# Row normalization and weight centring moved to ScalarE, one GpSimd task to VectorE, and a new order of steps, in a Nyström attention block with an expert FFN

## The chip, the cores and the metric

The kernel runs on one core of one Trainium2 chip. Such a core has five engines that run side by side, each working through its own instructions in order: TensorE (PE in the profile, its weight loads PEld), VectorE (DVE), ScalarE (ACT), GpSimd (POOL) and SyncE (SP), which here issues the DMA transfers. Engines wait for each other through semaphores. Matrix products land in PSUM, which other engines must empty before TensorE can write there again; everything else lies in SBUF.

The metric is the time of one execution in device microseconds. The kernel before was timed in three runs.

## The reference

The input is x of shape (16, 1024, 256) in float32: 16 batches of 1024 rows. Two sublayers follow each other, each with a normalization in front of it and one behind it:

```python
x = x + _layernorm(_L0_attn_ref(_layernorm(x), w_qkv, w_proj))
x = x + _layernorm(_L0_ffn_ref(_layernorm(x), W_base, b_base, Wd1, bd1, Wd2, bd2, Wa_down, ba_down, Wa_up, ba_up))
```

The attention has 16 heads of width 16 and 64 landmarks. Its landmarks are means over 16 neighbouring rows, and the inverse is an iteration of six steps:

```python
Q_l = Q.reshape(b, H, M, n // M, HD).mean(axis=-2)
K_l = K.reshape(b, H, M, n // M, HD).mean(axis=-2)
kernel1 = softmax(Q @ K_l^T); kernel2 = softmax(Q_l @ K_l^T); kernel3 = softmax(Q_l @ K^T)
SV = (kernel1 @ iterative_inv(kernel2)) @ (kernel3 @ V)
out = SV @ w_proj
```

The feed-forward part tries 8 small autoencoders (256 to 64 to 256) on the 1024 rows, picks the one with the least reconstruction loss, and adds that expert's adapter to a base projection. (The reference reads 16 batches of 1024 rows here; the loss is a mean over a batch's rows.)

```python
h = relu(x @ Wd1[e] + bd1[e]);  recon = h @ Wd2[e] + bd2[e]
losses = mean((recon - x) ** 2);  idx = argmin over e
a = relu(x @ Wa_down[idx] + ba_down[idx])
return x @ W_base + b_base + a @ Wa_up[idx] + ba_up[idx]
```

A layernorm here has no gain and no bias: (x - mean) / sqrt(var + 1e-5). Since the results of both sublayers are normalized again along the row, the kernel centres the weights that produce them (each row of `w_proj`, `W_base`, the chosen `Wa_up` and the bias rows loses its mean), so that the results have mean zero and only a variance is left to be found.

## The kernel before

Each batch passes four stages, written as Python generators. A generator yields at each *step*, and what stands between two yields is emitted in one piece.

- **Stage a** (`stage_a`, line 446): Q, K and V from the normalized rows. Steps `qk` (line 475: 64 matmuls each, two for Q and two for K; ScalarE copies at line 483, VectorE sums landmarks at line 489), `v` (line 500), `bd` (landmark matrices), `max` (line 547 with VectorE's maxima at line 556), `mcol` and `mrow` (the maxima split into three bfloat16 parts and turned), `e3` (lines 567 and 578, exponential on ScalarE at line 588), `ut` (line 604), `u`. The next batch's statistics and normalization (`stats` and `xn`) run inside it.
- **Stage p** (`stage_p`, line 664): the 64 by 64 inverse for all heads as one serial chain; `k2`, `k2n`, `sums`, `kv0`, then six rounds of `l` (line 698 and ScalarE's copy at line 780), `h` (VectorE, line 783) and `q` (line 698 and VectorE, line 787), then `end`.
- **Stage c** (`stage_c`, line 799): the queries' softmax (`max`: line 823 with VectorE's maxima at line 831; `mt`; `e1`: lines 862 and 870 with the exponential at line 880), the weighted values (`sv`: line 891), the projection (`po`: line 926), the residual addition (`out`: line 411). Its generator starts with the step `weights`, `prepare_c` (line 295), which centres `wproj_sb`.
- **Stage d** (`stage_d1` and `stage_d2`): statistics and normalization (`stats`, `xn`), the turn of the rows (`xt`), the eight experts (`ht`: line 999; `df`: line 1029, VectorE's difference at line 1037, two squares on ScalarE at line 1040), the choice (`pe`, `gather`, and an index read by SyncE that starts the loads of the expert's weights, `wup`), then `a`, `po` (line 1158) and `out`. Batch 0 starts with the step `weights`, `prepare_d` (line 302): three small transposes of bias rows on TensorE, three copies on ScalarE, and the centring of `wbase_sb` and the bias rows on VectorE.

Rows are normalized in `rows_normalized` (line 382), once per 512 rows: four tiles of 128 rows by 256, each by one `tensor_scalar` on VectorE (`normalized`, line 346). In stage a a VectorE transpose of the same 512 rows follows. The mean `mv` comes from VectorE (line 364), the reciprocal root `rstd` from two GpSimd instructions (`rstd_of`, line 367). There are 16 batches with two halves in each of two places: 64 such steps.

`in_parts` (line 338) splits float32 values into three bfloat16 parts with four instructions (copy, subtract, copy, subtract) on the engine that it is given; the queries' maxima in stage c are split on GpSimd (line 839).

Five streams of steps exist: stage a, stage p, stage c, stage d for all batches but the last but one, and stage d for that one. The string `ORDER` says which stream goes next; it has 1648 digits, and each engine gets its instructions in that order. The string `PAIRS` says which of four PSUM buffers (two banks each) every product takes, in the same order. Both were worked out ahead of time and are part of the program:

```python
order, emitted = [int(k) for k in ORDER], streams()
with tc.manual_schedule(engines={PE, Activation, DVE, Pool}):
    for k in order:
        next(emitted[k], None)
```

All loads and stores go through SyncE's queue in the order of emission. At the start it holds the first rows (8 transfers of 128 KB), `w_qkv` four times over (12 of 256 KB), `w_proj` four times over (4 of 256 KB), the experts' weights (1024 KB in three), `W_base` (256 KB), then the small bias rows and the rows for the base bias.

In stage d `spare` puts matmuls without use in front of a wait of the last batch (20 ahead of the transposes of batch 15, 16 ahead of its adapter).

Of the kernel before, what the change touches and what calls it, by code (L numbers as in the profile page):

```python
# [8 lines left out]
F32 = mybir.dt.float32  # L9
I32 = mybir.dt.int32  # L10
BF16 = mybir.dt.bfloat16
AF = mybir.ActivationFunctionType
ALU = mybir.AluOpType
X = mybir.AxisListType.X
PSUM = bass.MemoryType.PSUM

P = 128
# [1 line left out]
N_ITER = 6  # L19
PARTS = 3  # L20
ORDER = (
    "0000020000012000000000000011000000012110130011010010110121010110120101201100000122120122020000202012"
    "0112120112312013021310332001312132013303102333301301000133100030113003000330101102121023130112012213"
    "3201313001213030003201201000002133200020003312203013013023020111001022113212210302232033030100333133"
    "0133133310333333210313001012213311221030211331112100103322303030230200002312013003102223312301000133"
    "3313103333223133333130231300122133112213211030203001033221303030202033130010221022302331223133330321"
    "0333313010003333332103013001022131311221031021312330013322030302020012311100102303003022233113010001"
    "3331330210013313323233313330213123002122330001301233233322030301332331233132121331133231333331331223"
    "3331302003200210123021312010301200100020133200020003312203013033032331233132121333313321333311113333"
    "3202300122033211202133222101023010120100001010100101330001022303330302011203133112311120331231122133"  # L30
    "3322321333100110202130301230220113312013332031300000131312303030012013330303303311123123313212313332"
    "3112231333223213333101300131033110230132011003201200100020133200020001011223033303010200203023112030"
    "0302223312310100333132231010001333002210013322233321333211001330221030313113311130330200203232323300"
    "3122133223201201333331012013133313123331321233120332010313000010213001330012013330303303311110200112"
    "0012003102331300100033332232033323232333333211033101023032022302331001133230122033030113321323133123"
    "3113313213331313321212333331301120013011232132112321220102031020010033200330013023323302031211212223"
    "3231333131231133331323331321133122313122311312113121133212331224424422442224224422244444224244444442"
    "344423333334333443333343343333333433443333244333"
)
PAIRS = (  # L40
    "0123012301230123012301230123012301203120312032103120312031203120310321032013201320123102310321032103"
    "2013201323012301230123012301230123012301203120312013201320132013203120310231021032103210321032103231"
    "0231023102310231032103210321023102310231203120312031203120312031023102310231023012301203102310321023"
    "1023102310231203120132031203120312031203013203120310231021302103210321032103210321032103201320310231"
    "0231023102310213021320132013201320132013201312023103210320132013201320132013201320132013201302103210"
    "3210321032103210321032103210231023012301232031320132031203102301230123012301230123012310231023103210"
    "3210321032103201320123012301302130213021302102310213102310321032013201320132013210321032103210321032"
    "1032103120312031203120310231021032103212031203210321032103210321032103120312031230123012301230123012"
    "3102312031203120312031203123012301230123013201320132012301230123102310231023102310321032103210312031"
    "0231023102310231023102310231203120313201320132013120310231023120312031203120310231023103210321032103"  # L50
    "2103201320132013210321032103210321032103120312031203213021032103210321032103210321032103210321032103"
    "2130213012301230123012302132013203120123012301230123012132013201320132012301320132013203120312031203"
    "1203120132013201302130213021302130213012130213021302130213021030213032103201320132012301230120312031"
    "2031203120132013201320132103210231023102310231023102310232102310321032130213021302130213021302130213"
    "0123012301230132013201321032103210321032103210312301230123013210321032103120312031203120230123010231"
    "2031203120312031203120312031203102310231302103210321032103210321032013201320312031203120312031203102"
    "3102310231021302132012301230123021"
)


# [20 lines left out]
def kernel(  # L81
# [17 lines left out]
    nc = tc.nc  # L99
    NB, N, D = x.shape  # L100
# [3 lines left out]
    NC = D // P  # L104
    ND = D // 32
# [3 lines left out]
    E, _, R = wa_down.shape  # L109
# [20 lines left out]
    def rows32(p):  # L130
        return slice(32 * p, 32 * p + 32)
# [17 lines left out]
    def buf4k(tag, shape, name, bufs=2):  # L149

        return work.tile(shape, F32, tag=tag, name=name, bufs=bufs)
# [35 lines left out]
    wproj_sb = const.tile([P, ND, D], F32, name="wproj_sb")  # L187
# [67 lines left out]
    for c in range(NC):  # L255
        for r in range(2):
            j = 2 * c + r
# [37 lines left out]
    def prepare_c():  # L295
        yield go(("c", 0, "weights"), [("a", 0, "qk", 0, 0)])
        mean = small.tile([P, ND], F32, tag="means", name="means", bufs=1)
        nc.vector.tensor_reduce(mean, wproj_sb, X, ALU.add)
        nc.vector.tensor_scalar(mean, mean, 1.0 / D, None, ALU.mult)
        nc.vector.tensor_tensor(wproj_sb, wproj_sb, last(mean, D), ALU.subtract)  # L300

    def prepare_d():
        yield go(
# [39 lines left out]
            if q + 1 < PARTS:  # L343
                engine.tensor_copy(dst(q), rest)

    def normalized(dst, src, mv, rstd, i):
        nc.vector.tensor_scalar(dst, src, mv[:, i, 0:1], rstd[:, i : i + 1], ALU.subtract, ALU.mult)

    def go(name, follows):
        return name, follows

# [24 lines left out]
    def rows_normalized(b, at, src_of, stats, dst_of, turned_to=None):  # L382

        for h in range(NT // 4):
            yield go((at, b, "xn", h), [(at, b, "stats", h)])
            src, dst = src_of(h), dst_of(h)
            for j in range(4):
                normalized(dst[:, j, :], src[:, j, :], *stats[h], j)
            if turned_to is not None:
                nc.vector.transpose(  # L390
                    turned_to(h).rearrange("p (k t) c -> p t k c", t=4), dst.rearrange("p t (k c) -> p t k c", c=32)
                )
# [406 lines left out]
    def stage_c(b):  # L799
# [13 lines left out]
        def max_of(n, t0):  # L813

            if t0 == 0:
                most[n] = small.tile([P, 4, 4, 2 * NC], F32, tag="most1", name=f"most1_{b}_{n}", bufs=1)
            mx = most[n]
            psc = [two_banks([P, 2, 2, NC, P], f"psc1_{b}_{n}_{t0}_{g}") for g in range(PC // 2)]
            for c in range(NC):
                for t in range(2):  # L820
                    cols = slice((4 * n + t0 + t) * P, (4 * n + t0 + t + 1) * P)
                    for p in range(PC):
                        nc.tensor.matmul(  # L823
                            psc[p // 2][:, p % 2, t, c, :],
                            lhsT=qt[rows32(p), c, cols],
                            rhs=bd[rows32(p), NC + c, :, :].rearrange("f r l -> f (r l)"),
                            start=True,
                            stop=True,
                        )
            for g in range(PC // 2):  # L830
                nc.vector.tensor_reduce(  # L831
                    mx[:, t0 : t0 + 2, 2 * g : 2 * g + 2].rearrange("x t p j -> x p t j"),
                    psc[g].rearrange("x p t c (r l) -> x p t (c r) l", r=2),
                    X,
                    ALU.max,
                )
            if t0:
                by_row = maxima.rearrange("x t (p j) -> x t p j", p=4)
                in_parts(
                    nc.gpsimd, lambda q: by_row[:, :, :, q * 2 * NC : (q + 1) * 2 * NC], mx, mx  # L840
                )

        def before_rows(n):
# [364 lines left out]
    for k in order:  # L1208
        name, follows = stretches[k][place[k]]
# [50 lines left out]
```

## Time and profile before

| what | value |
|---|---|
| runs | 1941.35, 1941.46, 1944.79 us; median 1941.46 |
| profiled execution, time | 1940.27 us |
| profiled execution, span | 1938.1 us |
| mean granted TensorE clock | 0.99 |
| GpSimd busy | 212.1 us (11%) |
| moved by DMA | 64.30 MB, 33 GB/s over the span |
| first matmul starts at | 15.37 us |

The span is the time from the first to the last instruction in the profile; the execution takes 2.2 us more. Busy time is the time in which an engine executes; matmuls are pipelined, so that a busy TensorE isn't always one at its full rate. A line of a group reads: source line, engine, operation, tile written and read, shapes, count, then busy us in total and mean ns of one, then the idle time of the engine in front of these instructions and what ended it. A line of a timeline reads: start in us, length in us, engine, source line, operation, tiles, count, and in brackets the idle time of the engine before it and its releaser.

The largest groups outside TensorE are the squares of the reconstruction error on ScalarE (line 1040, 362.7 us) and the differences on VectorE (line 1037, 298.7 us), then VectorE's two maxima (lines 831 and 556, 150.2 and 149.8 us). One table load of ScalarE stands at the start (1.28 us).

### The profile page before, as it was taken

The page shows a single profiled execution, that of the slowest core. Times are in us where ns is not written, and L with a number is a line of the kernel's source. Part 1 is how long each engine was busy: PE and PEld are TensorE (multiplying, and loading weights), DVE is VectorE, ACT ScalarE, POOL GpSimd, SP SyncE. Part 2 cuts the span into 40 slices and gives each one's busy share as a digit, 9 for nine tenths or more (in the row PEclk, how much of TensorE's full clock was granted, in tenths as well). Part 3 has the DMA queues.
Part 4 walks back from the last instruction along what each step waited for, and adds up shares of the span by engine and source line. Part 5 has one row for each costly group of instructions (what it writes and reads, how often), then busy time and mean ns, then how long its engine had stood idle before and what let it go on. Part 6 is the DMA issues. An engine that isn't in the chain of part 4 may idle for free.

```text
span 1938.1 us, 81528 instructions
## 1 busy us (share of the span) xinstructions
PE 1844.0 (95%) x37175; PEld 1265.7 (65%) x37175; DVE 1511.4 (78%) x2805; ACT 1133.1 (58%) x2434; POOL 212.1 (11%) x423
## 2 busy tenths in 40 slices
PE   6789999999999999999999999999999999989898
PEld 5667578567585766677676666866758485755544
DVE  6787878878788787787788887888788877686664
ACT  1243745573847557665655756557474667456576
POOL 1001001001110101101010010101101010010101
PEclk9899999999999999999999999999999999999899
DMA  8011011102020110111110111110201110010101
GB/s 203 3 25 25 3 28 47 24 18 56 7 67 3 51 24 12 40 29 46 28 34 15 29 45 28 46 24 8 67 7 46 24 51 2 7 46 7 45 6 48
DMA packets 65767, 64.30 MB, mean 33 GB/s; under 512 B 9244, under 2 KB 65424, under 8 KB 65424
## 3 DMA queue, kind: packets, MB, share of 16 engines
q1 hardware_dynamic: 65424, 59.11, 11.7%
q8 instruction: 291, 4.77, 1.0%
q14 instruction: 52, 0.43, 0.1%
HBM read 42.32 MB, written 16.78 MB: 30 GB/s over the span
## 4 chain that ended last, share of the span: by engine, by line
PE 78%; DVE 11%; ACT 5%; issue 2%; DMA 2%; POOL 1%; SPq 1%; DVEq 0%; POOLq 0%; ACTq 0%
PE ph L999 10%; PE pq L475 10%; PE pr L1029 10%; PE pf L1158 6%; PE pv L500 5%; PE po L926 5%; PE psv L891 4%; PE psct L862 3%; PE psc L823 3%; PE psm L547 3%; PE pxl L698 3%; PE psc L578 3%; PE pxq L698 3%; PE put L604 2%; DVE mx L556 2%
## 5 line engine op out<-in xcount | busy, mean ns | idle before, releaser
L1040 ACT ACTIVATE df<-df,bd_sb 128x512 f32<-128x512 f32 x512 | 362.7, 711 | 80.8 <-DVE df L1037 80.6
L1037 DVE TENSOR_TENSOR df<-pr,xt_d 128x1024 f32<-128x1024 f32 x256 | 298.7, 1215 | 58.2 <-PE pr L1029 45.6
L475 PE MATMUL pq<-xa,wqkv_sb 32*128 32x256 f32 x4096 | 242.5, 382 | 15.6 <-DVE xa L390 15.4
L1029 PE MATMUL pr<-ht,wd_sb 64*64 64x512 f32 x2048 | 245.6, 599 | 1.0 <-ACT ht L1007 0.2
L999 PE MATMUL ph<-xt_d,wd_sb 128*128 128x512 f32 x512 | 236.5, 604 | 2.1 <-issue 0.9
L475 PEld LDWEIGHTS pq<-xa,wqkv_sb 32*128 32x128 f32 x4096 | 219.4, 187 | 28.9 <-DVE xa L390 15.4
L556 DVE TENSOR_REDUCE mx<-psm 128x2 f32<-128x1024 f32 x128 | 149.8, 1217 | 37.4 <-PE psm L547 36.9
L999 PEld LDWEIGHTS ph<-xt_d,wd_sb 128*128 128x128 f32 x512 | 92.0, 189 | 116.2 <-issue 94.4
L831 DVE TENSOR_REDUCE most<-psc 128x16 f32<-128x1024 f32 x128 | 150.2, 1216 | 14.1 <-PE psc L823 13.9
L880 ACT ACTIVATE e<-psct 128x1024 f32<-128x1024 f32 x128 | 123.8, 1019 | 60.9 <-PE psct L870 60.6
L1029 PEld LDWEIGHTS pr<-ht,wd_sb 64*64 64x64 f32 x2048 | 67.6, 132 | 120.5 <-issue 56.4
L588 ACT ACTIVATE e<-psc 128x1024 f32<-128x1024 f32 x128 | 122.9, 1025 | 31.4 <-PE psc L578 30.9
L926 PE MATMUL po<-wproj_sb,svn 32*128 32x256 f32 x2048 | 126.9, 380 | 1.5 <-DVE svn L962 1.4
L1007 ACT ACTIVATE ht<-ph,bd_sb 128x1024 f32<-128x1024 f32 x64 | 70.9, 1108 | 93.7 <-PE ph L999 93.5
L500 PE MATMUL pv<-wqkv_sb,xa 32*128 32x256 f32 x2048 | 124.7, 379 | 0.1
L926 PEld LDWEIGHTS po<-wproj_sb,svn 32*128 32x128 f32 x2048 | 108.7, 185 | 19.4 <-DVE df L1037 4.9
L1158 PE MATMUL pf<-wbase_sb,xt_d 128*128 128x256 f32 x512 | 120.0, 388 | 0.0
L500 PEld LDWEIGHTS pv<-wqkv_sb,xa 32*128 32x128 f32 x2048 | 109.3, 185 | 6.9 <-issue 1.0
L1158 PEld LDWEIGHTS pf<-wbase_sb,xt_d 128*128 128x128 f32 x512 | 95.3, 191 | 22.7 <-issue 10.9
L783 DVE SCALAR_TENSOR_TENSOR q<-qw,eye 128x512 f32<-128x512 f32 x96 | 65.2, 679 | 45.1 <-ACT qw L780 44.7
L787 DVE SCALAR_TENSOR_TENSOR xw<-xw,pxq 128x640 f32<-128x640 f32 x96 | 69.7, 726 | 39.2 <-PE pxq L698 38.4
L1040 ACT ACTIVATION_READ_ACCUMULATOR df<-df,bd_sb 128x1 f32 x512 | 96.7, 189 | 0.0
(185 smaller groups left out, 3054.7 us busy)
## 6 DMA issues: line engine op xcount, KB each, us to landing
x<-in_L_attn_x_dram SPq DMA_DIRECT2D x16, 1024.0 KB
xa<-in_L_attn_x_dram SPq DMA_DIRECT2D x60, 256.0 KB
out_dram<-y_d SPq DMA_DIRECT2D x30, 512.0 KB
wqkv_sb<-in_L_attn_w_qkv_dram SPq DMA_DIRECT2D x12, 256.0 KB
wup<-in_L_ffn_Wa_up_dram SPq DMA_DIRECT2D x30, 64.0 KB
xa<-in_L_attn_x_dram SPq DMA_DIRECT2D x8, 128.0 KB
wproj_sb<-in_L_attn_w_proj_dram SPq DMA_DIRECT2D x4, 256.0 KB
out_dram<-y_d SPq DMA_DIRECT2D x4, 256.0 KB
```

The source lines that it names most:

```text
L475: nc.tensor.matmul(pq[g // 2][:, g % 2, 0 : N // 4], lhsT=wqkv_sb[rows32(g), k, f0 : f0 + P], rhs=turned[rows32(g), k], start=(k == 0), st ...
L500: nc.tensor.matmul(pv[g // 2][:, g % 2, 0:D], lhsT=turned[rows32(g), k, t0 // 4, :], rhs=wqkv_sb[rows32(g), k, 2 * D : 3 * D], start=(k == 0),
L556: nc.vector.tensor_reduce(mx3[:, n, q : q + 2], psc[g], X, ALU.max)
L588: nc.scalar.activation(e, psc[g], AF.Exp)
L831: nc.vector.tensor_reduce(mx[:, t0 : t0 + 2, 2 * g : 2 * g + 2].rearrange("x t p j -> x p t j"), psc[g].rearrange("x p t c (r l) -> x p t ...
L880: nc.scalar.activation(e, psc[g], AF.Exp)
L926: nc.tensor.matmul(po[g // 2][:, g % 2, 0:D], lhsT=svt[rows32(g), k, :], rhs=wproj_sb[rows32(g), k, :], start=(k == 0), stop=(k == ND - 1),)
L999: nc.tensor.matmul(ph[:, n, :], lhsT=wd1_sb[:, k, 2 * i : 2 * i + 2, :].rearrange("p e h -> p (e h)"), rhs=xt[:, k, n * 512 : (n + 1) * 51 ...
L1029: nc.tensor.matmul(pr[to, r, :], lhsT=wd2_sb[half, i, k * P + 64 * f : k * P + 64 * f + 64], rhs=ht[half, cols], start=True, stop=True,)
L1037: nc.vector.tensor_tensor(df, pr, middle(xt[:, k, cols], 2), ALU.subtract)
L1040: nc.scalar.activation(df[:, r, :], df[:, r, :], AF.Square, bias=bd2_sb[:, e, k : k + 1], accum_out=part[:, e, k * NW + n : k * NW + n + 1],)
L1158: nc.tensor.matmul(banks[j // 2][:, j % 2, :], lhsT=xt[:, k, cols], rhs=wbase_sb[:, k, :], start=False, stop=(j % 2 == 1 and k == NC - 1),)
```

## The change

Four things change.

1. `rows_normalized` no longer calls `normalized`. For each 512 rows VectorE computes a `shift` of 128 x 4 values, minus mean times `rstd`, and ScalarE normalizes each of the four tiles with one activation (identity, scale `rstd` and bias `shift`, both one value per row). The four VectorE instructions fall away; the transpose of stage a stays on VectorE.
2. `prepare_c` centres `wproj_sb` on ScalarE: eight activations into a scrap tile, which write minus the mean through their accumulator, then eight that add it.
3. In the last batch the queries' maxima are split into parts on VectorE; in the others still on GpSimd.
4. `ORDER` and `PAIRS` are new strings; the steps themselves, and what each step has to follow, are the same. Among other things the step `weights` of stage d moves ahead of the fourth projection of batch 0, `weights` of stage c moves behind `mcol` of batch 0, and in the tail the experts of batches 14 and 15 are interleaved earlier and the second output group of batch 14 moves behind the gather of batch 15.

```diff
 ORDER = (
-    "0000020000012000000000000011000000012110130011010010110121010110120101201100000122120122020000202012"
...
+    "0000000300000000022020000001020020002010110110101100100111011010010101000001101112212120020020202012"
...
 )
 PAIRS = (
-    "0123012301230123012301230123012301203120312032103120312031203120310321032013201320123102310321032103"
...
+    "0123012301230123012301230123012301231023102310231023102310231023102312031023102130213021302130213021"
...
 )
     def prepare_c():
         yield go(("c", 0, "weights"), [("a", 0, "qk", 0, 0)])
         mean = small.tile([P, ND], F32, tag="means", name="means", bufs=1)
-        nc.vector.tensor_reduce(mean, wproj_sb, X, ALU.add)
-        nc.vector.tensor_scalar(mean, mean, 1.0 / D, None, ALU.mult)
-        nc.vector.tensor_tensor(wproj_sb, wproj_sb, last(mean, D), ALU.subtract)
+        rows = buf4k("yc", [P, D], "rows")
+        for k in range(ND):
+            nc.scalar.activation(rows, wproj_sb[:, k, :], AF.Copy, scale=-1.0 / D, accum_out=mean[:, k : k + 1])
+        for k in range(ND):
+            nc.scalar.activation(wproj_sb[:, k, :], wproj_sb[:, k, :], AF.Identity, bias=mean[:, k : k + 1])
...
-    def normalized(dst, src, mv, rstd, i):
-        nc.vector.tensor_scalar(dst, src, mv[:, i, 0:1], rstd[:, i : i + 1], ALU.subtract, ALU.mult)
...
             yield go((at, b, "xn", h), [(at, b, "stats", h)])
             src, dst = src_of(h), dst_of(h)
+            mv, rstd = stats[h]
+            shift = small.tile([P, 4], F32, tag="shift", name=f"shift_{at}{b}_{h}")
+            nc.vector.scalar_tensor_tensor(shift, mv[:, :, 0], -1.0, rstd, ALU.mult, ALU.mult)
             for j in range(4):
-                normalized(dst[:, j, :], src[:, j, :], *stats[h], j)
+                nc.scalar.activation(
+                    dst[:, j, :], src[:, j, :], AF.Identity, bias=shift[:, j : j + 1], scale=rstd[:, j : j + 1]
+                )
...
                 in_parts(
-                    nc.gpsimd, lambda q: by_row[:, :, :, q * 2 * NC : (q + 1) * 2 * NC], mx, mx
+                    nc.vector if b == LAST else nc.gpsimd, lambda q: by_row[:, :, :, q * 2 * NC : (q + 1) * 2 * NC], mx, mx
                 )
```

More of the change, by code (lines that the diff above doesn't have):

```diff
@@ L21 @@
 ORDER = (
-    "0000020000012000000000000011000000012110130011010010110121010110120101201100000122120122020000202012"
[L23 to L36, printed above, removed]
@@ L37 @@
-    "3231333131231133331323331321133122313122311312113121133212331224424422442224224422244444224244444442"
-    "344423333334333443333343343333333433443333244333"
+    "0000000300000000022020000001020020002010110110101100100111011010010101000001101112212120020020202012"
+    "2131021022003300300331003101033130000133100010133103123333203002033010310121211122102133310022033120"
+    "2130213120103001200100012010000302110233303122030131320101120111001023112031010302331301000133331302"
+    "2201013331322333313330213123021223310103121311123100103322303000200320303132020100301222331230331332"
@@ new lines @@
+    "3200133331310333333201313001022131030223233001013233122030131320020111001023112031010302223310300003"
+    "3332333331232133333130321300122133002203211330010323131220303101312020111001023112031010302223312301"
+    "0131333232010333133033333312033001022131030223211312330010122013310130103200311200233003021033123010"
+    "3133132131001312333223233133133201033110022031223203021132001201130130330201101331020301232231003102"
+    "0233103000033332232333333313331321033001022131030223233001013233122030320132001111001023112031010302"
@@ new lines @@
+    "2233123010001331333103333223133333312033101022031030223233001013233122030320112001213100103112031003"
+    "1022233123010001333313103333223133333312033001022131032203203301012331322030320132001121100102113213"
+    "1021310123322323332023302010003331330133122133332003030102133121310330012013330303202001211003023123"
+    "1122101031233232331321020332010003331303133122333320031312103311010031213001201133033300332100020023"
+    "1120302302023130311031333223213333130033313331203103001022131030223233001013233122030133203323112113"
@@ L39 @@
+    "3313311233123133331313332331023220301300121020231321122102113001030332003301023302103101123323211123"
+    "3123133331332233322323331213123312223312313211322131313322124421412114422242422222224424344423344334"
+    "434443434344433343334433333433433334334332444333"
 )
 PAIRS = (
-    "0123012301230123012301230123012301203120312032103120312031203120310321032013201320123102310321032103"
-    "2013201323012301230123012301230123012301203120312013201320132013203120310231021032103210321032103231"
@@ L43 @@
[L43 to L57, printed above, removed]
+    "0123012301230123012301230123012301231023102310231023102310231023102312031023102130213021302130213021"
@@ new lines @@
+    "3021321030213023102310231023102310230213021302130213023102321032103210321032103210321032103210312031"
+    "2031230123012301023102310231203120310231023102313021302130213021302130213021302310231032103201320132"
+    "0132013021302310231023103210321032103210213021030213021302132031203120312031203120312031203120312302"
+    "1301230123012301230130213021302130213021303201302130231031203120132013201320132013210321031203123012"
+    "3012301230123012301320132013201230123012301231012302130230123012301230123012301230123102310213021320"
@@ new lines @@
+    "1320132013201320130213021302130213021302130213032120312023103120312031203120312031203120312031201320"
+    "1320132013201302130231023102310230123012301201320213201302131023102310231023102310231023102310231023"
+    "0123013201320132013201320130213021302130213013201032010321030213210321031203120312031203120132013210"
+    "3210231023102310231023103210320132013201320132013201312031023130210231023120312031203120312032103210"
+    "3120312013201320132013201302130231023102310231023102310123201320213012301230213021302130213021320132"
@@ new lines @@
+    "0132031203210321032103210321032103210312301230213012301230123012301302130213021302310231023102310321"
+    "0321032103120312031203120312031201320132102310230123102310231023102321032103210321032103210321032103"
+    "2103213021301230123012301231203120321032103210321032103102312013210321023123012301320132013201320132"
+    "1032103210321302301230123012301230123012301230120312031203210321302013021302130212301230123012031203"
+    "1203120132013201320132013201320132013120321203120312031203120312031230123102310231023102310231021301"
@@ L58 @@
+    "3201320132031203102310213012301320"
 )
```

## The prediction

> **What bounds the kernel now.** I read the busy shares and slices first, then the chain, then stretches, then single waits.
>
> ```profile
> PE 1844.0 (95%) x37175; PEld 1265.7 (65%) x37175; DVE 1511.4 (78%) x2805; ACT 1133.1 (58%) x2434; POOL 212.1 (11%) x423
> PE   6789999999999999999999999999999999989898
> PE 78%; DVE 11%; ACT 5%; issue 2%; DMA 2%; POOL 1%; SPq 1%; DVEq 0%; POOLq 0%; ACTq 0%
> ```
>
> TensorE is busy nearly everywhere, yet only 78% of the chain that ended last is TensorE's; 11% is VectorE's and 5% ScalarE's. So "busy" hides short waits inside a group of matmuls. To size them I price each kind of matmul by its densest run (192 of the Q/K projection took 10.57 us back to back, 8 of L999 3.63, 32 of L1029 3.60) and multiply by the counts: 1764 us of TensorE work against a span of 1938.1, so 174 us lost. By place: about 52 us before 172 us, 83 between 172 and 1675 us (1503 us hold 1420 of work), some 39 after.
>
> ```profile
> 0.00:20.00 20.00, 4.63 (x42) 4.63 (x46) 13.23 (x43) 1.28 (x1) 7.84 (x23) 1.00 0.95 211
> 20.00:40.00 20.00, 19.70 (x356) 18.84 (x353) 12.92 (x16) 6.04 (x11) 0.00 (x0) 1.00 0.86 207
> 40.00:60.00 20.00, 14.97 (x221) 9.99 (x217) 16.91 (x34) 4.30 (x6) 2.40 (x4) 0.83 0.34 76
> 1300.00:1400.00 100.00, 98.94 (x2092) 69.46 (x2092) 80.08 (x155) 63.40 (x140) 11.26 (x20) 1.00 0.14 36
> 1800.00:1820.00 20.00, 12.26 (x239) 9.03 (x240) 17.74 (x39) 6.39 (x7) 3.69 (x9) 0.66 0.25 79
> ```
>
> The columns after the length are busy us of PE, PEld, DVE, ACT, POOL, then the granted clock, the DMA share and GB/s. At 40 to 60 us and at 1800 to 1820 us VectorE is the busiest (16.9 and 17.7 of 20) while TensorE starves; in the middle VectorE has 20% to spare on average and ScalarE 37%.
>
> **The change, part by part.**
>
> *Rows normalized by ScalarE.* Each of 64 steps loses four subtract-multiplies on VectorE.
>
> ```profile
> L347 DVE TENSOR_SCALAR xn_d<-x,mv_d,rstd_d 128x256 f32<-128x256 f32 x128 | 43.6, 407 | 0.8 <-POOL rstd_d L371 0.8
> L347 DVE TENSOR_SCALAR xn_a<-xa,mv_a,rstd_a 128x256 f32<-128x256 f32 x128 | 43.5, 403 | 3.3 <-PE psc L578 3.3
> L423 ACT ACTIVATE svn<-y_c 128x256 f32<-128x256 f32 x128 | 53.7, 419 | 3.0
> ```
>
> VectorE sheds 43.6 + 43.5 = 87 us, 1.35 a step (four follow each other in 1.34 to 1.38), and gains a 128x4 shift of some 0.2 (128x8 instructions there take 0.15 to 0.23): net 1.15, over 64 steps 74 us. ScalarE gains four activations, a form the trace lacks. Upper bound 4 x 0.55 = 2.2 us, the squares of L423 with their accumulator reads (start to start 0.545); lower bound 1.2, since the second of two 128x512 copies (L483, two in 1.08, one 0.595) adds 0.49. I take 1.4, nearest to the square without its read (four at 0.33 and a 0.1 tail): 90 us over 64 steps.
>
> The Trainium skill speaks against this move: "ScalarE: Activation LUTs", Rules for kernel authors, wants add and multiply on VectorE, and "VectorE: DVE Perf Modes", The TRN2 errata, prices 256 fp32 elements at 400 ns on ScalarE against 194 on VectorE. By these pages VectorE would be relieved of only some 50 us; this case's trace shows 403 to 407 ns on VectorE and 382 to 419 on ScalarE, so the measurement decides.
>
> *What that is worth.* Both orders are written out in the kernels and arrange the same 1648 steps, so I price every step on each engine from the rows (PE/DVE/ACT us: Q or K projection 3.5/1.2/1.1; V 3.6/0/1.1; key maxima 1.1/2.3/0; weights e3 1.2/0/1.9; query maxima 1.1/2.3/0; e1 1.3/0/1.9; sv 1.2/1.1/0 and 1.25 DVE more for the turn; po 3.6/0/3.3; ht 3.6/0/1.1; df 0.9/1.2/1.4; d's po 5.0/0/3.2; out 0/1.7/0; stats 0/2.1/0; l 0.7/0/0.7; q 0.7/1.5/0). Then I slide a stretch holding 10 us of TensorE work (about what four PSUM buffers let it run ahead) along either order and add up by how much VectorE or ScalarE needs more than 10 us in it, per us of TensorE work. Before: start (first 120 us of work) 21.0, middle 77.5, end (last 224) 21.7. The middle meets the 83 us lost there, so 10 us is a fair length. After: 16.2, 64.3, 19.1. Of the middle, VectorE's excess falls from 65 to 47 and ScalarE's rises from 15 to 22. Gain -4.8, -13.2, -2.6: together -20.6. With 1.2 us a step the gain is 23, with 2.2 it is 5; with stretches of 5, 15, 20 and 30 us it is 24, 20, 15 and 5.
>
> *Start.* Before, VectorE centred the projection weights right behind the first projection.
>
> ```profile
> 27.28 2.29 DVE L298 TENSOR_REDUCE means<-wproj_sb 128x8 f32<-128x2048 f32 x1 [2.65 <-DMA wproj_sb<-in_L_attn_w_proj_dram]
> 28.03 0.42 SPq L198 DMA_DIRECT2D bd_rows<-in_L_ffn_bd_dram  x1
> 29.81 2.29 DVE L300 TENSOR_TENSOR wproj_sb<-wproj_sb,means 128x2048 f32<-128x2048 f32 x1
> 53.45 0.26 PE L632 MATMUL pm<-ident_b,maxima 128*128 128x128 bf16 x1 [4.50 <-DVE maxima L342]
> ```
>
> These 4.75 us leave VectorE; ScalarE gets eight activations with accumulators (8 x 0.545) and eight without (8 x 0.33), 7.0 us, after the V copies, in a gap of 13.2 us that ScalarE has before its first exponential at 56.6; without that cover 7.0 us would be added. Against it: the first normalization now crosses to ScalarE and back, so the first matmul comes later than 15.37 by two crossings less what the overlap saves, +0.8 (0 to 1.5). And step d-weights is moved from 81 us to ahead of the fourth projection: three small transposes of bias rows stand there in TensorE's queue, with 6.3 us of VectorE work (83.97 to 90.3). TensorE gets there at 29.2 + 0.8 = 30.0. The rows are issued at 28.0 to 29.8, behind 6.55 MB (8 x 128 + 12 x 256 + 4 x 256 + 1280 KB), which at 207 to 211 GB/s is through at 31.3, and another small load here takes 2.0 from issue to use (1916.43 to 1918.45): 33.3, a wait of +3 (0 to 6). Queued behind it is the whole of the fourth projection and V.
>
> The clock column reads 0.83 after 40 us and 0.66 at 1800; "TensorE: Matmul & The Clock Gate", Part 1, says a window of some 3.4 us without work halves the clock for as long, which would make this wait cost up to 1.7 us more; no row shows a wait of that length.
>
> *End.* The last batch's maxima parts go from GpSimd to VectorE.
>
> ```profile
> 1800.09 1.67 DVE L411 SCALAR_TENSOR_TENSOR y_d<-y_d,rstd_d_y,x 128x256 f32<-128x256 f32 x4 [2.56 <-POOL rstd_d_y L371]
> 1801.67 4.61 DVE L831 TENSOR_REDUCE most<-psc 128x16 f32<-128x1024 f32 x4
> 1806.35 0.24 POOL L340 CAST maxima<-most 128x64 bf16<-128x64 f32 x1 [6.30 <-DVE most L831]
> 1807.36 0.32 POOL L342 TENSOR_TENSOR maxima<-most,maxima 128x64 bf16<-128x64 f32 x1
> 1807.74 0.61 PE L853 MATMUL pm<-ident_b,maxima 128*128 128x128 bf16 x4 [9.00 <-POOL maxima L342]
> ```
>
> The wait of 9.00 us bears GpSimd's name, but its four instructions are the last 1.39 us of it; 1.67 and 4.61 are VectorE's. On VectorE four 128x64 instructions take about 1.0 (0.17 each at 128x8, 0.29 at 128x256): -0.4 and less crossing, -0.5 each, -1 for two. The new order still has the residual addition in front of these maxima, so the rest of the wait stays. At the very end the second output group of batch 14 (5 us of matmuls) moves behind the gather of batch 15 and covers the 0.74 us that TensorE waited for the expert's weights: -0.7.
>
> **Sum.** -20.6 + 0.8 + 3 - 1 - 0.7 = -18.5 on the span: 1919.6. The profiled execution had 1940.27, 2.2 above its span, and lies 1.2 below the median of the runs. So about 1922, 1923 on the median's footing.
>
> **Rivals.** (1) *ScalarE's queue becomes the bound, slower.* An in-order ScalarE empties most PSUM buffers. Place: the 62 normalization steps after the first two, where projections and po wait behind. Price: 1.4 us, and 1.35 where the two GpSimd instructions of rstd are not done when its turn comes, so 2.75 a step. It eats the gain once 7 of the 62 steps hold TensorE up; with 16 of them (a quarter), 44 - 18.5 = +25: 1965. For it: ScalarE's excess in long stretches grows (20 us stretches: 3 to 9 in the middle). Against it: 58% busy before, about 63% after, and stats mostly stand a projection ahead.
> (2) *Hidden anyway.* The middle's losses belong to serial chains (xw, l, product, copy, q), which the change doesn't shorten; then -13.2 drops out: 1935. For it: several of the longest TensorE waits name q and l. Against it: the sum by stretches explains 78 of 83 us without them.
> (3) *More than counted.* The order also spaces the chains: between q and the next l, 14 of 80 places had under 2 us of other TensorE work, now 7. If losses outside the sum (174 - 120 = 54 us) shrink by a third too, -18 more: 1904.
>
> **How the numbers follow.** Forecast 0.45, its own range 1908 to 1935 (bounds 23 and 5, wait 0 to 6). Rival 1: 0.25; rival 2: 0.12; rival 3: 0.18. A measurement tells a change from none at about 0.2%, 4 us. Faster: 0.45 + 0.18 + 0.08 of rival 2 = 0.71; same 0.05; slower 0.24. The range 1900 to 1952 leaves out some 0.06 below and the worse half of rival 1 above.
>
> **What would show it.** Four 128x256 activations in 1.2 to 2.2 us; VectorE's busy time near 1511 - 87 + 13 - 5 = 1432, ScalarE's near 1133 + 107 + 7, with TensorE's share of the chain above 78%; a wait of about 3 us at the bias transposes; the wait for the last batch's first maxima still above 7 us. Wrong would be: TensorE waiting for ScalarE's copies behind xn steps, a middle without gain, or a new wait in the first 80 us.

## The result, and the profile after

The changed kernel took 1971.94 us in the median of four runs (1965.60 to 1974.33), the kernel before 1943.12 in four beside it: a ratio of 1.0143, interval 1.0119 to 1.0167. By the ratio it is slower by 28 us, where a gain of 18.5 was forecast, and above the range (1900 to 1952). The profiled execution took 1970.83 us, with a span of 1968.8.

Busy engines, the slices of TensorE and the chain that ended last, from the page of the changed kernel:

```profile
PE 1854.7 (94%) x37175; PEld 1277.6 (65%) x37175; DVE 1433.9 (73%) x2618; ACT 1265.0 (64%) x2714; POOL 209.4 (11%) x415
PE   5879999999999999999999999999999999999798
PE 72%; ACT 11%; DVE 9%; issue 3%; DMA 2%; SPq 1%; POOL 1%; DVEq 0%; POOLq 0%; ACTq 0%
```

VectorE shed what it was to shed (1511.4 to 1433.9; 1432 forecast), and ScalarE took 132 us where 114 were forecast. TensorE's share of the chain fell from 78 to 72%, ScalarE's rose from 5 to 11%. The stretches shown before, here of the changed kernel (the stretch of the last maxima lies 20 us later; columns as before):

```profile
0.00:20.00 20.00, 2.66 (x24) 2.66 (x27) 10.80 (x37) 5.43 (x9) 7.74 (x23) 1.00 1.00 202
20.00:40.00 20.00, 17.14 (x297) 16.48 (x294) 7.57 (x15) 4.65 (x11) 0.00 (x0) 1.00 0.77 177
40.00:60.00 20.00, 17.68 (x215) 11.62 (x208) 18.02 (x28) 9.30 (x28) 0.00 (x0) 0.83 0.45 116
1300.00:1400.00 100.00, 97.39 (x1977) 68.19 (x1973) 74.55 (x142) 69.65 (x156) 12.62 (x25) 1.00 0.09 26
1820.00:1840.00 20.00, 10.49 (x227) 7.18 (x229) 16.42 (x37) 8.05 (x18) 4.02 (x6) 0.74 0.31 96
```

Between 1300 and 1400 us VectorE is busy for 74.6 us instead of 80.1 and ScalarE for 69.7 of 100, yet TensorE does no more work: it issues 1977 matmuls instead of 2092. (The two orders have different matmuls there. Priced by kind, the difference is some 2 us of work, an estimate.) So the time freed on VectorE bought nothing here; something waits. The groups that the move made:

```profile
L384 ACT ACTIVATE xn_a<-xa,shift_a,rstd_a 128x256 f32<-128x256 f32 x128 | 66.3, 590 | 20.9 <-DVE shift_a L382 14.1 <-issue 6.0
L384 ACT ACTIVATE xn_d<-x,shift_d,rstd_d 128x256 f32<-128x256 f32 x128 | 66.0, 590 | 22.4 <-DVE shift_d L382 22.3
L388 DVE STREAM_TRANSPOSE xa<-xn_a 128x1024 f32<-128x1024 f32 x32 | 39.8, 1245 | 82.8 <-ACT xn_a L384 82.8
```

The number after the second bar is the engine's idle time in front of these instructions. ScalarE waited 36 us for VectorE's shifts, and VectorE 82.8 us (2.6 a transpose) for ScalarE's rows; before, VectorE idled 1.1 us there. The 82.8 us are about as much as the move freed on VectorE (74 us by the prediction). One place of it, VectorE first and then ScalarE, from the timeline of the changed kernel (four squares on ScalarE between the copy and the last line are left out):

```profile
896.19 1.25 DVE L960 STREAM_TRANSPOSE svn<-svn 128x1024 f32<-128x1024 f32 x1
897.35 0.12 DVE L382 SCALAR_TENSOR_TENSOR shift_a<-mv_a,rstd_a 128x4 f32<-128x4 f32 x1
899.67 1.25 DVE L388 STREAM_TRANSPOSE xa<-xn_a 128x1024 f32<-128x1024 f32 x1 [2.19 <-ACT xn_a L384]
900.84 0.12 DVE L382 SCALAR_TENSOR_TENSOR shift_a<-mv_a,rstd_a 128x4 f32<-128x4 f32 x1
905.21 1.25 DVE L388 STREAM_TRANSPOSE xa<-xn_a 128x1024 f32<-128x1024 f32 x1 [4.25 <-ACT xn_a L384]
```

```profile
897.56 2.08 ACT L384 ACTIVATE xn_a<-xa,shift_a,rstd_a 128x256 f32<-128x256 f32 x4 [2.54 <-issue]
900.04 1.01 ACT L418 COPY y_d<-pf 128x1024 f32<-128x1024 f32 x1 [0.40 <-PE pf L1156]
903.12 2.06 ACT L384 ACTIVATE xn_a<-xa,shift_a,rstd_a 128x256 f32<-128x256 f32 x4
```

VectorE makes the shift and meets the transpose of the same rows next in its queue. It must stand still until ScalarE has done four activations (2.08 us), and the second time until ScalarE has also done a copy and four squares that stand ahead in ScalarE's queue.

To place the loss I count matmuls by line in stretches of 25 us and price them as in the prediction; that tells when a kernel has done a given amount of TensorE work. How much later than the kernel before ten of the other kernels get there (us, estimates from one profiled execution each, good to some 2 us, and to 4 at 1650, where the orders do different kinds of work):

| kernel | 100 us of work | 300 | 1000 | 1400 | 1650 | 1760 | measured ratio |
|---|---|---|---|---|---|---|---|
| changed kernel | 9 | 18 | 19 | 18 | 27 | 30 | 1.0143 |
| e1 | 9 | 14 | 21 | 20 | 26 | 31 | 1.0139 |
| e2 | 7 | 32 | 89 | 138 | 147 | 153 | 1.0811 |
| e3 | 6 | 10 | 6 | 1 | 1 | 8 | 1.0054 |
| e4 | 13 | 23 | 34 | 36 | 41 | 48 | 1.0258 |
| e6 | -1 | 8 | 28 | 41 | 47 | 52 | 1.0294 |
| e7 | -1 | 5 | 3 | -2 | -1 | 5 | 1.0044 |
| e10 | 10 | 16 | 12 | 9 | 6 | 16 | 1.0098 |
| e11 | 6 | 8 | 2 | -4 | 1 | 3 | 1.0038 |
| e13 | 0 | -1 | -7 | -9 | -7 | -7 | 0.9964 |

In the changed kernel the first 300 us of work lose 18, the next 1350 lose 8 where 13 were to be gained, and the end loses 4. Nearly all of those 8 are lost after 1400; between 300 and 1400 us of work the kernel neither gains nor loses.

### The profile page after: what moved, and what is told of

Same layout as the page of the kernel before. It is cut to its first block, busy times and chain, and to the rows that moved or that the text cites. A ratio compares the mean times of both kernels' runs of the same rounds, so it can differ in the third digit from the quotient of the medians.

```text
span 1968.8 us, 81541 instructions
## 1 busy us (share of the span) xinstructions
PE 1854.7 (94%) x37175; PEld 1277.6 (65%) x37175; DVE 1433.9 (73%) x2618; ACT 1265.0 (64%) x2714; POOL 209.4 (11%) x415
## 4 chain that ended last, share of the span: by engine, by line
PE 72%; ACT 11%; DVE 9%; issue 3%; DMA 2%; SPq 1%; POOL 1%; DVEq 0%; POOLq 0%; ACTq 0%
PE ph L997 11%; PE pq L473 10%; PE pr L1027 9%; PE pv L498 5%; PE pf L1156 5%; PE po L924 4%; ACT df L1038 4%; PE psv L889 3%; PE psc L821 3%; PE psm L545 3%; PE psct L860 2%; PE pxq L696 2%; PE pxl L696 2%; DVE mx L554 2%; PE psc L576 2%
## 5 line engine op out<-in xcount | busy, mean ns | idle before, releaser
L473 PEld LDWEIGHTS pq<-xa,wqkv_sb 32*128 32x128 f32 x4096 | 222.2, 188 | 29.1 <-DVE xa L388 17.3
L889 PEld LDWEIGHTS psv<-w_bd,e 128*32 128x32 f32 x8192 | 80.0, 110 | 46.2 <-ACT e L878 15.1
L889 PE MATMUL psv<-w_bd,e 128*32 128x34 f32 x8192 | 89.0, 199 | 17.3 <-issue 7.8
L388 DVE STREAM_TRANSPOSE xa<-xn_a 128x1024 f32<-128x1024 f32 x32 | 39.8, 1245 | 82.8 <-ACT xn_a L384 82.8
```

Source lines behind the costliest of these rows:

```text
L473: nc.tensor.matmul(pq[g // 2][:, g % 2, 0 : N // 4], lhsT=wqkv_sb[rows32(g), k, f0 : f0 + P], rhs=turned[rows32(g), k], start=(k == 0), st ...
L889: nc.tensor.matmul(psv[rows32(g), j // 2, col : col + 2 * (HD + 1)], lhsT=es[p // 2][:, p % 2, g * P + 32 * j : g * P + 32 * j + 32], rhs= ...
```

## The experiments

Fourteen kernels ran. Times are medians; the kernel before, run beside them on the same chip, had 1940.3 (e1, e2, e3, e5), 1937.3 (e4, e6, e7, e9), 1938.0 (e10 to e13) and 1937.6 (e14, e15); comparisons between groups go by the ratio to it. The first two set two theories against each other: M, that the move to ScalarE costs the time, through VectorE's wait at the transposes; and O, that the new order itself does.

**e1: new order, rows on VectorE.**

```diff
-                nc.scalar.activation(dst[:, j, :], src[:, j, :], AF.Identity, bias=shift[:, j : j + 1], scale=rstd[:, j : j + 1])
+                nc.vector.tensor_scalar(dst[:, j, :], src[:, j, :], mv[:, j, 0:1], rstd[:, j : j + 1], ALU.subtract, ALU.mult)
```

> The kernel after with the normalization put back on VectorE (its four subtract-multiplies, 0.41 us each); the new order, the weights on ScalarE and the last maxima on VectorE stay. Theory M (the move is the loss: VectorE stands 82.8 us in front of its transposes in stage a, and a step costs ScalarE 2.07 us): VectorE's wait at the transpose goes to about nothing, and the time falls from 1972 to 1945 or less. Rival O (the new order itself is worse, at the start and in the tail): 1960 to 1975, as after.

Measured 1966.3, ratio 1.0139 (1.0122 to 1.0156). With the rows back on VectorE the new order is as slow as with them on ScalarE. For an order that was to suit rows on ScalarE this doesn't clear the move, so e2 is the other half.

**e2: old order, all rows on ScalarE** (the kernel before with the new `rows_normalized` alone).

> The kernel before with nothing changed but the normalization on ScalarE (shift on VectorE, four activations); old order. Theory M: the old order gets the same wait of VectorE at the transpose, some 2.6 us in each of 32 places, and the time rises from 1943 by 20 or more, to 1963 or above. Rival O: 1938 to 1950, since VectorE loses 87 us of work and ScalarE has room.

Measured 2095.0, ratio 1.0811 (1.0793 to 1.0830): the move alone costs 157 us, far more than expected. A group and a wait of e2:

```profile
L395 DVE STREAM_TRANSPOSE xa<-xn_a 128x1024 f32<-128x1024 f32 x32 | 39.9, 1245 | 137.2 <-ACT xn_a L391 137.2
```

```profile
PE pu L658 <- DVE ut L619: 51.3, 10, 7.6
PE pxq L703 <- DVE q L788: 11.7, 11, 3.1
```

VectorE stands 137 us in front of the transposes, and TensorE waits for small VectorE additions that are queued behind (51.3 us for `ut`, 3.9 before). The move is very dear where the order is not made for it, and the new order is dear by itself: neither theory alone.

**e3: changed kernel, stage a's rows (those turned by VectorE) back on VectorE, stage d's on ScalarE. e4: the other way round.**

```diff
+            if turned_to is not None:   # e4: is None
+                for j in range(4):
+                    nc.vector.tensor_scalar(dst[:, j, :], src[:, j, :], mv[:, j, 0:1], rstd[:, j : j + 1], ALU.subtract, ALU.mult)
+            else:
...
```

> The kernel after with only stage a's normalization back on VectorE; stage d's stays on ScalarE. Theory M with the transpose as the place: the wait of 82.8 us is gone, and the time falls by 15 to 30, to 1942 to 1957, most of what the full return brings. A second theory, ScalarE's longer queue (2.07 us a step in both stages): half of what the full return brings. Rival O: within 5 us of 1972.

> The mirror image of the run with stage a on VectorE (1949.5): new order, stage d's rows normalized on VectorE, stage a's, which are turned behind it, on ScalarE. Theory W (the price lies in VectorE's transposes, which wait in VectorE's queue until ScalarE is done): the 83 us of idle time in front of the transposes stay, and VectorE has 43 us more to do: 1975 to 2000. Rival Q (the price lies in ScalarE's queue, whichever rows it normalizes): as many activations leave ScalarE as in the mirror image, so again 1943 to 1957.

e3: 1949.5, ratio 1.0054 (1.0036 to 1.0071). e4: 1987.1, ratio 1.0258 (1.0238 to 1.0277), with 82.3 us of idle time in front of the transposes. Both times fall where the transposes as the place had them (e3's theory M, e4's W). But e3's expectation took its gain to be most of what a full return brings, and the full return (e1) brought next to nothing, since it also takes stage d's rows off ScalarE. Under the new order, taking stage a's rows off ScalarE gains 17 us (ratio 1.0143 to 1.0054), taking stage d's off loses 22.

**e5: both halves' activations in the first step, both transposes in the second**, so that VectorE has other work between shift and transpose.

```diff
+            elif h == 0:
+                dsts = {i: scaled(i) for i in range(NT // 4)}
+            else:
+                for i, dst in dsts.items():
+                    nc.vector.transpose(turned_to(i).rearrange(...), dst.rearrange(...))
```

> The kernel after with the same work on the same engines, but in stage a both halves are normalized at the first of the two steps and both transposes stand at the second, so that what lies between them in the order runs on VectorE while ScalarE works. Theory M with the wait as its mechanism: VectorE's idle time at the transposes falls from 82.8 to under 40 us and the time by 8 to 20, to 1952 to 1964. ScalarE's queue as the cause: no gain or a loss, since 4.1 us of activations stand in one piece (1970 to 1980). Rival O: within 5 us of 1972.

Measured 1993.4, ratio 1.0272 (1.0251 to 1.0293): slower, a miss, above every band of the expectation. VectorE's waits in e5, then TensorE's:

```profile
DVE rec L907 <- PE psv L898: 69.8, 20, 9.1
DVE xa L397 <- ACT xn_a L383: 39.4, 28, 4.9
```

```profile
PE pf L1152 <- ACT a_t L1141: 16.8, 6, 3.4
```

The wait at the transposes was halved (82.8 to 39.4), but eight activations in a row hold ScalarE for 4.1 us, and waits elsewhere grew: TensorE waits 16.8 us for the adapter's `a_t` instead of 6.1, and VectorE 69.8 us for `psv` instead of 29.1. Here the idle time at the transposes couldn't be bought back with a longer piece on ScalarE.

**e6: old order, only stage d's rows on ScalarE.** No VectorE transpose follows them.

> The kernel before with one edit: only stage d's rows, which TensorE turns, are normalized on ScalarE. With both stages' rows there the old order took 2095. Theory W (the transposes behind it on VectorE are the price): there is none in stage d, so 1930 to 1965. Rival Q (ScalarE's queue, whichever rows): half of the 155 us, 2000 to 2030.

Measured 1992.6, ratio 1.0294 (1.0272 to 1.0316): theory W missed by 28 us, and the rival's band was not reached either. The group of e6's activations, and then VectorE and ScalarE between 334 and 344 us, show what W lacked:

```profile
L393 ACT ACTIVATE xn_d<-x,shift_d,rstd_d 128x256 f32<-128x256 f32 x128 | 65.7, 591 | 41.2 <-DVE shift_d L390 41.2
```

```profile
336.39 1.22 DVE L498 TENSOR_REDUCE lsum<-kt 128x64 f32<-128x1024 f32 x1 [3.10 <-ACT kt L492]
337.52 2.35 DVE L840 TENSOR_REDUCE most<-psc 128x16 f32<-128x1024 f32 x2
339.79 0.15 DVE L390 SCALAR_TENSOR_TENSOR shift_d<-mv_d,rstd_d 128x4 f32<-128x4 f32 x1
343.04 1.22 DVE L498 TENSOR_REDUCE lsum<-kt 128x64 f32<-128x1024 f32 x1 [3.10 <-ACT kt L492]
```

```profile
335.30 1.05 ACT L492 ACTIVATE kt<-pq 128x512 f32<-128x512 f32 x2
339.97 2.08 ACT L393 ACTIVATE xn_d<-x,shift_d,rstd_d 128x256 f32<-128x256 f32 x4 [3.62 <-DVE shift_d L390]
341.95 1.05 ACT L492 ACTIVATE kt<-pq 128x512 f32<-128x512 f32 x2
```

Read it as a ring: VectorE's landmark sum waits for ScalarE's copy `kt`; two maxima follow it; then comes the shift of 0.15 us; ScalarE, which idled 3.62 us for the shift, does the activations and only then the next `kt`, for which VectorE has idled 3.10. One turn takes 6.65 us (336.39 to 343.04). In the kernel before, the same two copies start at 329.32 and 333.83, 4.51 us apart. A tiny instruction on the wrong queue ties the two engines together here, so that they work by turns. I call this theory S; e12 tests it.

**e7: the new order only between its 264th and its 1479th step**, both places at which the two orders have emitted the same steps; old order ahead and behind, projection weights on VectorE, rows as in e3. **e9: e3 with the old order from the 1480th step on.** The digits of `PAIRS` behind a seam are renamed so that the least recently used buffer comes next.

> New order only between its 264th and its 1479th step (two places at which both orders have emitted the same steps); the steps ahead of them and behind them in the old order, the projection weights centred on VectorE as before; stage a's rows on VectorE, stage d's on ScalarE, last maxima on VectorE. By the amount of TensorE work done, the run with the new order throughout and the same engines was 10 us late after the start, 1 to 2 late ahead of the end and 8 late at the end. If these losses belong to the order of the start and of the end: 1928 to 1937. If they are owed by what the start and the end hand over (a queue that is fuller, a lead that is used up in the middle): 1944 to 1955.

> The run with stage a on VectorE and stage d on ScalarE (1949.5), with only the steps from the 1480th on in the old order. If the end's order costs 6 to 8 us: 1940 to 1945. If it costs nothing and the lateness came from ahead: 1947 to 1952.

e7: 1945.7, ratio 1.0044 (1.0028 to 1.0059). e9: 1952.0, ratio 1.0072 (1.0054 to 1.0090). Both fall into the rival's band, e9 at its upper edge. The old start works (e7 is 5 us late after 300 us of work, e3 10), but the old end gives nothing while the last two batches' rows stay on ScalarE: 6 us go between 1650 and 1760 us of work in e7, where TensorE's transposes of these rows wait 6.6 us (4.7 for ScalarE's `e`, 1.9 for `xn_d`; 1.9 in all in the kernel before).

**e10 to e13: the shift on GpSimd**, by two instructions right behind `rstd` in the statistics step. e10 is the changed kernel so, e11 is e3, e12 is e6, e13 is e7, the latter with stage d's rows of batches 14 and 15 on VectorE.

```diff
+        rstd = rstd_of(mv[:, :, 1], 1.0, name, tag)
+        nc.gpsimd.tensor_scalar(shift, mv[:, :, 0], -1.0, 0.0, ALU.mult, ALU.add)
+        nc.gpsimd.tensor_tensor(shift, shift, rstd, ALU.mult)
...
-            nc.vector.scalar_tensor_tensor(shift, mv[:, :, 0], -1.0, rstd, ALU.mult, ALU.mult)
```

> The changed kernel with one edit: the shift (minus mean times rstd, 128x4) is made by two GpSimd instructions right behind rstd, in the statistics step, and no longer by VectorE in the normalization step. In the changed kernel ScalarE idled 36.4 us (14.1 + 22.3) in front of its normalizations because VectorE's shift stood in VectorE's queue behind other work. Theory S (this loop, VectorE to ScalarE and back to VectorE, is a price of its own): that idle time falls below 10 us, the 82.8 us in front of the transposes to 50 to 68, time 1938 to 1960. Rival (the activations would wait for their place all the same, so that the time only moves to the next wait): 1963 to 1978.

> The run with stage a's rows on VectorE and stage d's on ScalarE (new order, 1949.5, 1.0054 of before) with stage d's shift on GpSimd. ScalarE idled 20.7 us for it there. Theory S: 1928 to 1942, ratio 0.992 to 1.001. Rival: 1945 to 1953, ratio 1.003 to 1.007.

> The kernel before with stage d's rows on ScalarE (old order, 1992.6, 1.0294 of before) with their shift on GpSimd. ScalarE idled 41.2 us for it there, against 52 us that the move cost. Theory S: most of the 52 us go, 1940 to 1965. Rival (ScalarE's queue holds the copies of the projections up by 2 us a step, whoever makes the shift): 1975 to 1995.

> The run with the new order in the middle alone and both ends old (1945.7, 1.0044 of before), with stage d's shift on GpSimd, and stage d's rows of the last two batches on VectorE, as before. ScalarE idled 29.0 us for the shift there; the end lost 6 us while the rows of the last two batches were on ScalarE. Theory S: 1918 to 1936, ratio below 1.000. Rival (as in the other runs of this set): 1939 to 1948, ratio 1.001 to 1.005.

| kernel | time | ratio to before (interval) | twin with the shift on VectorE |
|---|---|---|---|
| e10 | 1956.6 | 1.0098 (1.0083 to 1.0113) | 1.0143 |
| e11 | 1944.9 | 1.0038 (1.0025 to 1.0050) | 1.0054 |
| e12 | 1961.0 | 1.0109 (1.0092 to 1.0125) | 1.0294 |
| e13 | 1931.8 | 0.9964 (0.9952 to 0.9977) | 1.0044 |

e10, e12 and e13 fall where theory S had them. e11 gains 0.16% with overlapping intervals and lands in its rival's band by ratio: with the new order and no turned rows on ScalarE, the waits for the shift (20.7 us in e3) cost little. In e12 ScalarE's wait for the shift falls from 41.2 to 9.8 us, and 36 of e6's 57 us come back; what the other 21 are is not shown. The groups of e10:

```profile
L386 ACT ACTIVATE xn_d<-x,shift_d,rstd_d 128x256 f32<-128x256 f32 x128 | 66.1, 597 | 1.1 <-POOL shift_d L361 1.0
L386 ACT ACTIVATE xn_a<-xa,shift_a,rstd_a 128x256 f32<-128x256 f32 x128 | 66.1, 596 | 3.4 <-POOL shift_a L361 3.0
L390 DVE STREAM_TRANSPOSE xa<-xn_a 128x1024 f32<-128x1024 f32 x32 | 39.8, 1244 | 70.1 <-ACT xn_a L386 70.1
```

ScalarE's 36 us of waiting fall to 4, and the middle, where the changed kernel loses 8 us, now gains 7 to 10 (16 us late at 300 us of work, 9 at 1400, 6 at 1650); the 70 us in front of the transposes stay, slightly above the 50 to 68 expected. e13 is faster than both kernels, than the one before by 0.36%. It differs from e7 in two edits, so how much each gave is not parted.

**e14: step `weights` of stage d back behind batch 1's first projection. e15: the projection weights on VectorE again, at their new place.** Each undoes one thing in the changed kernel (e14 with the digits of `PAIRS` renamed).

> The changed kernel with the step weights of stage d moved back behind batch 1's first projection, where the kernel before has it. In the changed kernel its bias transposes waited 2.9 us for their DMA, but its 6.3 us of VectorE work also left the crowded stretch at 80 to 90 us. If the wait is the whole of it, 3 us less: 1965 to 1970. If the VectorE work then collides with the chain of batch 0 as it did before: 1971 to 1978. If the early step set off the 18 us of the start: 1952 to 1960.

> The changed kernel with the projection weights centred by VectorE again, at their new place behind mcol of batch 0. The prediction had ScalarE do it in a gap, at no cost, and VectorE relieved of 4.75 us at a place where it is the busiest engine. If so, this run is slower by up to 5 us: 1972 to 1978. If the ScalarE version holds something up (the exponentials behind it, which the next steps need): 1962 to 1970.

e14: 1969.9, ratio 1.0159 (1.0139 to 1.0178). e15: 1971.6, ratio 1.0178 (1.0161 to 1.0195). The intervals touch or overlap that of the changed kernel (1.0119 to 1.0167), so e14 shows no gain and e15 at most a small loss. In e15 VectorE's 4.75 us make the kernel 7 to 8 us later at 100 us of work than the changed kernel (16.7 against 9.2), and from 1500 us on the profiles of both, and of e14, stand within 2 us of each other: an early loss need not reach the end.

## Why the prediction was wrong

**The sum by stretches failed**, the step that gave -20.6 us. It slid a stretch of 10 us along the order and counted what VectorE or ScalarE had to do in it beyond 10 us. That sees engine time alone, and lets every engine work in the stretch in any order. Redone with the measured price of an activation step it gives some -9 us for the changed kernel, -16 for e2 and -10 for e6 (estimates, good to some 3 us); measured were +28, +157 and +57. It explained 78 of the 83 us lost in the middle of the old order, but that agreement was no proof: in the kernel before nothing crosses engines between a row's normalization and its transpose, so a sum without a term for crossings could fit it. Crossings are what the runs show in its place: in the changed kernel VectorE stands still at each transpose (82.8 us in all) and ScalarE at each shift (36 us), and in e6 copies and sums queue behind. With the shift alone taken out of VectorE's queue, 36 of e6's 57 us come back (e12) and 9 of the changed kernel's 28 (e10).

**Crossings are not the whole of it.** By the ratios, the changed kernel's 28 us are 27 for the new order alone (e1), 16 less for stage d's rows on ScalarE (e1 to e3) and 17 more for stage a's (e3 to the changed kernel). In the other sequence it is 23 more for stage a's (e1 to e4) and 22 less for stage d's (each good to some 4 us, by the intervals). In e1 no row crosses engines, yet the sum, roughly redone for it, gives -4 us (an estimate) where +27 were measured. Stage d's rows, which cost 57 us under the old order, gain under the new one, not far from what the sum has for them there (some -11). So under the new order the sum failed in what that order is worth by itself, and in stage a's rows (some +3 by the sum). Why the new order loses by itself stays open.

**The clock takes part.** The granted clock of the profiled executions was 0.990 before, 0.982 in the changed kernel and 0.981 in e1. Behind TensorE's wait of 9.00 us the kernel before had a clock of 0.50 (1807 to 1811 us), and the same eight matmuls took nearly twice as long there as at 1.00 (1815 to 1820 us):

```profile
1808.28 2.09 PE L862 MATMUL psct<-qt,bd 32*128 32x512 f32 x8
1816.17 1.14 PE L862 MATMUL psct<-qt,bd 32*128 32x512 f32 x8
```

By the traces, TensorE was busy at 0.50 for 27 us before, 56 in the changed kernel and 63 in e1. Up to half of what was added, 15 of the changed kernel's 28 us (an estimate), may then be matmuls slowed behind waits and not the waits themselves; no run parts the two. The prediction found no row with a wait that long; its own rows show waits of 4.50 and 9.00 us, and behind the first, too, the clock was 0.50 (53.4 to 57.0 us). The wait that it asked about, at the bias rows, left the clock at 1.00 (28 to 40 us).

**The price of a normalization step was mis-sized**: 1.4 us, bounds 1.2 to 2.2, measured 2.07. The squares that served as the nearest row have constants for scale and bias (419 ns); with a bias per row the instruction takes 492 ns (L302, eight in 3.28 us with overlap: 0.41 each), with scale and bias per row 586 to 590. The Trainium skill says so: "ScalarE: Activation LUTs", What ACT_TABLE_LOAD costs, adds about 93 ns for every per-partition operand, on 186 ns and 0.833 ns an element. From these figures, an estimate for 256 elements is 585 ns, and 2.06 us for four with the page's overlap of 93 ns; this trace agrees to 0.02 us. The prediction cited another page, whose 400 ns lack that term, and took its 1.4 us from the rows of the trace. The size alone would have cost the forecast some 12 us, not its sign.

**The start** was to gain 1.0 us (-4.8 + 0.8 + 3) and lost 18 (9 by 100 us of work; the prediction's start ends at 120). The early bias rows, from the timeline of the changed kernel:

```profile
31.52 0.19 PE L309 MATMUL bias_ps<-ident,bd_rows 4*128 4x4 f32 x1 [1.19 <-DMA bd_rows<-in_L_ffn_bd_dram]
33.38 0.23 PE L310 MATMUL bias_ps<-ident,bd_rows 16*128 16x16 f32 x1 [1.68 <-DMA bd_rows<-in_L_ffn_bd_dram]
```

They waited 2.9 us, and 3 were predicted, with the rows there by 33.3. But e14 takes this wait out and gains nothing: the wait was right, and no price of it is seen at the end. (e14 also puts 6.3 us of VectorE's work back where they stood, so the two aren't parted.) The first matmul started at 17.34, 2.0 after before and not 0.8, since VectorE holds shift, transpose, shift, transpose in this order and each transpose waited 2.14 us. Centring `wproj_sb` on ScalarE ran from 45.2 to 52.7 in a gap, as predicted, and e15 bears out that it costs nothing. Of the 18 us, e1 loses 14 with all rows on VectorE. e10 against e11 puts some 7 on stage a's rows on ScalarE, and e7 against e3 puts 5 on the order of the first 264 steps with the weights; what is left is not parted.

**The end** was to gain 4.3 us (2.6 + 1 + 0.7) and lost 4. TensorE's waits there in the changed kernel:

```profile
PE psv L889 <- ACT e L878: 5.3, 4, 3.0
PE pm L851 <- DVE maxima L344: 3.0, 1, 3.0
PE pxq L696 <- DVE most L829: 2.5, 1, 2.5
PE psc L821 <- ACT qw L778: 1.8, 1, 1.8
```

The wait for the last maxima fell from 9.0 to 3.0, not to 8.5, since the new order has other matmuls (`pxq`) ahead of it, which now wait 2.5 us for the same maxima. In e7, where the old end stands around it, it is 8.6: the parts on VectorE give 0.4, and 0.5 was predicted. But the last batch's inverse and weighted values now stand closer to their own makers: waits of 2.5, 1.8, 3.0 and more appear that weren't there. The wait of 0.7 for the last expert's weights is gone, as predicted.

**The rivals.** Rival 1 had the sign and the place (normalization steps in ScalarE's queue) and priced 25 us for 16 held steps; 28 were measured. That nearness is luck: the 25 hold the -18.5 of the sum that failed, and e1, with no normalization in ScalarE's queue, is as slow. Its mechanism is only half of what ran: what it says queues behind ScalarE (projections, `po`) is seen in e6, and the shift and the transposes in VectorE's queue, the other half of the ring, stood in no rival. Rival 2's serial chains were tested by no run, and rival 3's gain didn't come. Two named signs were there at first sight: TensorE's share of the chain, which was to stay above 78%, was 72%, and the middle was without gain.

## What to carry to other kernels

Before an operation is moved to another engine, follow its operands in and its results out through both in-order queues: here a consumer that stayed on the old engine right behind it turned freed time into idle time, whatever the sums of busy time said. A small helper of the moved work (here a 128x4 product) belonged where its inputs were made early and the queue was empty, not on the engine that was to be relieved; that choice alone was worth 0.45% (e10) and 1.85% (e12), and in e11 0.16%, which is not clear of the noise. And a change of order and a change of engine are to be measured apart, since each was worth more than 1% here, and the same move (stage d's rows) lost under one order and gained under the other.

## What the runs showed that I had not expected

- One 128x256 activation took 417 to 419 ns with constants (382 to 383 where it read PSUM), 492 ns with a bias per row and 586 to 590 ns with scale and bias per row; VectorE's `tensor_scalar` with two per-row operands on the same tile 403 to 407 ns.
- GpSimd made the 128x4 shift in 0.20 us for each of two instructions, against 0.14 to 0.15 in one on VectorE, so moving it there cost 0.4 us a step of an engine that is 11% busy.
- A loss of 5 to 8 us in the first 300 us of work (e15 against the changed kernel) was gone at 1500; what absorbed it was not followed.
